# Pacing the preparation of entries in a neighbour-quantile kernel: late steps made good, first entries at shorter distances, sorts begun with the lists

## The chip, the cores and the metric

The kernel runs on one core of a Trainium2 chip, with its engines TensorE (PE), VectorE (DVE), ScalarE (ACT), GpSimd (POOL) and SyncE (SP, which issues transfers). The metric is the device time of one execution in microseconds; lower is better.

## The reference, cut to what matters

There are 16 graphs ("entries") of 1024 nodes with 64 features. Four layers follow each other, each with a residual and a layer norm:

```python
x = ln(x + mlp0(x, adj @ x))            # layer 0: tanh MLP on node and message
x = ln(x + (adj / deg) @ x)             # layer 1
x = ln(x + mlp2(x + quantiles(x, nd)))  # layer 2
x = ln(x + mlp3(x + quantiles(x, nd)))  # layer 3

# nd: neighbours left after a dilation; every skip-th neighbour of a node is removed, both ways
sv  = sort(where(nd, x[None], big))     # per node and feature, over its neighbours
agg = 0.25 * q(sv, .25) + 0.5 * q(sv, .5) + 0.25 * q(sv, .75)   # interpolated between two ranks
```

A node keeps between 1 and 33 neighbours, itself included. The neighbour set depends on the adjacency alone, so layers 2 and 3 use the same lists.

## The kernel before, in words

**Preparation of an entry b.** Three generators write its instructions piece by piece.

- `features` (L403) loads `x` and the adjacency, computes layers 0 and 1 (TensorE tiles `px`, `pd`, `pa`), makes the 0/1 matrix `near` on VectorE, writes the features to a table in DRAM and splits them into three bf16 parts. It sets `e.near`, then `e.parts[0]`.
- `lists` (L488) counts ranks with matmuls (`pr`), finds the removed neighbours (`takes`, then `e.taken`), sorts the nodes of the entry by their number of neighbours (`order`), packs the neighbour numbers (`pk`, then `e.packed`), and takes the largest eight at a time into the lists `e.idx` (`best`, `idx`; then `e.listed`).
- `ordered` (L634) is started by `lists` once `order` is there. It puts the features into node order (`e.xs[0]`, tile `x2s`), makes `place` and `none` for the longest lists, the quantile weights `e.wts`, and a check of the list lengths whose last instruction writes `over`.

**Rounds.** `sort_round(k)` handles layer 2 of entry k and layer 3 of entry k-2 together; there are 18 rounds, and rounds 0, 1, 16 and 17 have only one of the two. Nodes stand in eight tiles of 128, in the order of their list length. For seven of the tiles GpSimd gathers neighbours from the table with indirect transfers into a ring of 72 slots (`got_s`, by `fetch`, L886). For the eighth and longest, TensorE picks them with one-hot matrices (`fill`, L726: `hot` on VectorE, `pgk` on TensorE). VectorE sorts every tile with a network of min and max (`got`, `other`). `weigh` (L753) multiplies by `e.wts` and sums up; it also marks the ring slots as free. `finish_round` (L908) runs the MLP of the finished layers; the results of layer 2 are scattered to a second table and read back by `read_back` (L814).

**Order of the work.** On VectorE, ScalarE and TensorE the program's order is the one in which Python writes the instructions; GpSimd and SyncE are ordered by the scheduler of the compiler. `Weave` (L825) decides the order. Its clock is the planned VectorE time so far (`Metered`, L193: 0.13 us and a share by size for each instruction) and time skipped. A generator yields the distance to its next step in these microseconds. After every sort instruction `catch_up` takes the steps that are due. `step` sets the next due time:

```python
work[0] = max(self.now() - work[2], work[0]) + next(work[1])   # work[2] is the lag
```

With a lag of 0 the next distance counts from the moment at which the step was taken; with a lag of 4.0 (only `fill` has one) from its due time, as long as it was less than 4 us late. If a round needs something that is not there, `advance` takes the next step at once, whatever its due time, and the clock jumps.

`prepare` (L872) starts `features(b)` when entry b-1 has its `taken` and b is at most two past the current round, and `lists(b)` when b-1 is `listed`. A round's sorts of entry k are written only when `ready(k)` (L882): all three generators of the entry have ended.

Of the kernel before, what the change touches and what calls it, by code (L numbers as in the profile page):

```python
# [12 lines left out]
F32 = mybir.dt.float32  # L13
# [8 lines left out]
P = 128  # L22
# [190 lines left out]
def adj_resnorm_kernel(ctx: ExitStack, tc: tile.TileContext, x, adj_t, nodemask, w01, b01, w02, b02,  # L213
                       w21, b21, w22, b22, w31, b31, w32, b32, out):
    nc = tc.nc
    B, N, C = x.shape
    NT = N // P
# [3 lines left out]
    s = SimpleNamespace()  # L221
# [78 lines left out]
    most_wanted = max(len(want) for want in wants)  # L300
    want_ids = const.tile([P, NT, most_wanted], F16, name="want_ids")
    nc.gpsimd.memset(want_ids, NEVER)
    for t, want in enumerate(wants):
        for first, m, stride, length in regular_runs(want):
            for r in range(m):
                k = first + r * stride
# [178 lines left out]
        yield from split(x2, parts, y)  # L485
        e.parts[0] = parts

    def lists(b, e):  # L488

        while e.near is None:  # L490
            yield 2
# [3 lines left out]
        half = s.work.tile([P, NT], I32, name="nb_half", bufs=1)  # L495
        m, dil, lim, cut_at = st[:, 0], st[:, 1], st[:, 2:4], st[:, 4:6]
# [57 lines left out]
        own = s.work.tile([P, NT, 3], F16, name="own", bufs=1)  # L554
# [37 lines left out]
        order = s.sets.tile([P, NT, N], BF, name="order", tag="takes")  # L592
        for t in range(NT):
            dve.tensor_scalar(order[:, t, :], slot, key[:, 2, t : t + 1], None, op0=ALU.is_equal)
            if t % 3 == 2:
                yield 2
        preparing[b].append(weave.add(ordered(b, e, order, own)))


        e.idx = s.feat.tile([P, NT, KS], I32, name="idx", bufs=5)  # L600
# [33 lines left out]
    def ordered(b, e, order, own):  # L634
# [49 lines left out]
        e.place = place  # L684

        e.none = s.feat.tile([KW - 1, P], BF, name="none", bufs=5)
        e.wts = s.feat.tile([P, NT, most_wanted], F32, name="wts", bufs=5)
        for h in range(NH):
            half = slice(h * G, (h + 1) * G)
            pn = s.psum.tile([P, G, P], F32, name="pn", tag="s", bufs=1)  # L690
            for q in range(G):
                nc.tensor.transpose(pn[:KW, q, :], sorted_own[:, h * G + q, :1].to_broadcast([P, KW]), ident)
            yield 7
            counted = s.work.tile([KW, G, P], F32, name="counted", bufs=1)
            dve.tensor_scalar(counted, pn[:KW], nth[:KW], None, op0=ALU.is_equal)
            if h == NH - 1:
                dve.tensor_scalar(e.none, pn[: KW - 1, G - 1, :], nth[: KW - 1], BIG, op0=ALU.is_le, op1=ALU.mult)
            pw = s.psum.tile([P, G, most_wanted], F32, name="pw", tag="s", bufs=1)
            for q in range(G):
                nc.tensor.matmul(pw[:, q, :], counted[:, q, :], weights[:KW, h * G + q, :], start=True, stop=True)  # L700
            yield 9
            nc.scalar.copy(e.wts[:, half, :], pw)

        pc = s.psum.tile([P, HALF], F32, name="pc", tag="s", bufs=1)
        nc.tensor.transpose(pc[:NT, :P], count, ident)
# [16 lines left out]
    def members(k):  # L722

        return [(m, b, entries[b]) for m, b in enumerate((k, k - 2)) if 0 <= b < B]

    def fill(k):  # L726

        while k and (k - 1, NT - 1) not in free:
            yield 1
        t = NT - 1  # L730
        size = SIZES[t]
        got = tails[k] = s.lists.tile([P, 2, size, C], F32, name="got", tag="got_l", bufs=1)
        for m, b, e in members(k):
            while e.parts[m] is None or e.xs[m] is None or e.place is None or e.none is None:
                yield 1
            nc.scalar.copy(got[:, m, 0, :], e.xs[m][:, t, :])
            for g in range(1, size, 8):
                pg = s.psum.tile([P, 8, C], F32, name="pgk", tag="f", bufs=1)
                for i in range(g, g + 8):
                    hot = s.lists.tile([P, NT, P], BF, name="hot", bufs=HOTS)  # L740
                    dve.tensor_scalar(hot, e.place, float(i), None, op0=ALU.is_equal)
                    whole = i < LEAST[t]
                    if not whole:
                        nc.tensor.matmul(pg[:, i - g, :], e.none,
                                         ident_b[: KW - 1, i - 1 : i].to_broadcast([KW - 1, C]), start=True, stop=False)
                    pick(pg[:, i - g, :], hot, e.parts[m], whole)
                    yield 2.1
                yield 2
                nc.scalar.copy(got[:, m, g : g + 8, :], pg)
                yield 0.5  # L750
            e.filled[m] = True

    def weigh(k, t, got, agg, which):  # L753

        want = wants[t]
        prods = got[:, :, : len(want), :]
        for i, slot_id in enumerate(want):
            for m, b, e in members(k):
                nc.scalar.activation(prods[:, m, i, :], got[:, m, slot_id, :], AF.Copy, scale=e.wts[:, t, i : i + 1])  # L759
            if i % 6 == 5:  # L760
                yield 3
        yield 13
        left = len(want)
        while left > 2:
            more = left // 2
            dve.tensor_add(prods[:, which, :more, :], prods[:, which, :more, :], prods[:, which, left - more : left, :])
            left -= more
        dve.tensor_add(agg[:, which, t, :], prods[:, which, 0, :], prods[:, which, 1, :])
        free.add((k, t))
# [55 lines left out]
    class Weave:  # L825
# [5 lines left out]
        def now(self):  # L831
            return dve.us + self.skipped

        def add(self, gen, lag=0.0):

            self.works.append([self.now(), gen, lag])
            return gen

        def step(self, work):
            try:  # L840
                work[0] = max(self.now() - work[2], work[0]) + next(work[1])
            except StopIteration:
                self.works.remove(work)

# [15 lines left out]
        def finish(self, gen):  # L860
            while self.runs(gen):
                self.advance()

    entries = [SimpleNamespace(near=None, taken=False, packed=False, listed=False, there=None, place=None, none=None,
                               parts=[None, None], xs=[None, None], filled=[False, False]) for _ in range(B)]
    weave = Weave()
    preparing, tails = {}, {}
    free, gots, room, holders = set(), [], [0], [None] * ROOM
    allowed = [1]
    order_of_tiles = [(k, t) for k in range(B + 2) for t in reversed(range(NT - 1))]  # L870
# [1 line left out]
    def prepare():  # L872

        for b in range(B):
            while b > allowed[0] or (b and not entries[b - 1].taken):
                yield 2
            preparing[b] = [weave.add(features(b, entries[b]))]
            while b and not entries[b - 1].listed:
                yield 2
            preparing[b].append(weave.add(lists(b, entries[b])))  # L880

    def ready(b):  # L882

        return len(preparing.get(b, ())) == 3 and not any(weave.runs(gen) for gen in preparing[b])

    def fetch(must=-1):  # L886

# [27 lines left out]
    def sort_round(k):  # L915

        if k >= 2:
            weave.finish(rounds[k - 2])
        filling = weave.add(fill(k), lag=4.0)
        first = members(k)[0][0]  # L920
        which = slice(first, first + len(members(k)))
        agg = s.feat.tile([P, 2, NT, C], F32, name="agg")
        sums = []
        for t in (*reversed(range(NT - 1)), NT - 1):
            if t == NT - 1:
                weave.finish(filling)
                got = tails[k]
            else:
                n = order_of_tiles.index((k, t))
                fetch(n)  # L930
                got = gots[n]
            other = s.lists.tile([P, 2, SIZES[t], C], F32, name="other", bufs=1)
            pair = got[:, which], other[:, which]
            for is_max, d, v, i, j, to in usual[t]:
                dve.tensor_tensor(cut_pair(pair[to], v, d if is_max else 0), cut_pair(pair[i], v),
                                  cut_pair(pair[j], v, d), op=ALU.max if is_max else ALU.min)
                weave.catch_up()
                fetch()
            if len(sums) >= 2:
                weave.finish(sums[-2])  # L940
            sums.append(weave.add(weigh(k, t, got, agg, which)))
            weave.catch_up()
        if k:
            weave.finish(rounds[k - 1])
        rounds.append(weave.add(finish_round(k, agg, sums)))

    with ExitStack() as main:
        s.feat = main.enter_context(tc.tile_pool(name="feat", bufs=2))
        s.work = main.enter_context(tc.tile_pool(name="work", bufs=2))
        s.sets = main.enter_context(tc.tile_pool(name="sets", bufs=1))  # L950
        s.lists = main.enter_context(tc.tile_pool(name="lists", bufs=1))
        s.psum = main.enter_context(tc.tile_pool(name="psum", bufs=1, space=bass.MemoryType.PSUM))
        engines = mybir.EngineType
        main.enter_context(tc.manual_schedule(engines={engines.DVE, engines.Activation, engines.PE}))
        weave.add(prepare())
        rounds = []
        ring = s.lists.tile([P, 2, ROOM, C], F32, name="got_s")
        for k in range(B + 2):
            allowed[0] = k + 2
            sort_round(k)  # L960
        for gen in rounds:
            weave.finish(gen)


    def layernorm(dst, y):
# [216 lines left out]
    with tc.If(nc.values_load(over_d[:, B:]) > 0):  # L1182
        with tc.For_i(0, B) as b:
            with tc.If(nc.values_load(over_d[:, ds(b, 1)]) > 0), ExitStack() as general:
# [9 lines left out]
                wts = s.feat.tile([P, NT, LONG], F32, name="wts")  # L1194
# [62 lines left out]
```

## Time and profile before

| | |
|---|---|
| device time, median of 3 runs | 5359.1 us (5350.06 to 5362.13) |
| span of the profiled run | 5360.1 us |
| mean granted TensorE clock | 0.754 |
| busy: DVE / PE / POOL / ACT | 4448.2 / 3801.1 / 3665.9 / 2309.6 us |
| indirect gathers on POOL | 2944, 1143 ns in the mean |
| `hot` on DVE | 1024 instructions, 438 ns in the mean |

Busy time is the time in which an engine executes; waits are not in it. Because three engines are written in a fixed order, an instruction that waits holds back all that stand behind it on its engine. VectorE's instructions all bear the line of the metering helper (L207), so they are told apart by the tile that they write. The ends of rounds 0 to 3, seen at the last `agg<-got` of each, are at about 411, 729, 1140 and 1450 us, round 14 ends at 4764, and rounds 15, 16 and 17 end at 5021, 5138 and 5319.

The times of the first four entries, of one tile each (first start to last end, us):

| tile, engine | entry 0 | entry 1 | entry 2 | entry 3 |
|---|---|---|---|---|
| `px`, PE | 22 to 53 | 141 to 192 | 365 to 436 | 688 to 755 |
| `takes`, DVE | 129 to 137 | 351 to 362 | 672 to 682 | 961 to 972 |
| `pk`, PE | 180 to 226 | 428 to 483 | 748 to 800 | 1051 to 1103 |
| `idx`, DVE | 198 to 233 | 447 to 489 | 767 to 807 | 1087 to 1127 |
| `over`, DVE (end) | 267 | 556 | 871 | 1166 |

### The profile page before, as it was taken

What the parts mean: (1) busy time and instruction counts of PE and PEld (TensorE: products, weight loads), DVE (VectorE), ACT (ScalarE), POOL (GpSimd) and SP (SyncE); (2) the same over time, 40 slices, a digit from 0 to 9 for tenths busy, and PEclk for the clock granted to TensorE, in tenths of its full rate; (3) what the DMA queues carried; (4) which work ended last, traced back from release to release, by engine and by line L of the source; (5) the groups of instructions that cost most, each with busy time, mean ns of one, the idle gap of its engine ahead of it and who ended that gap; (6) DMA issues with size and microseconds to landing.
All of it is one profiled execution on the core that took longest, in us unless ns stands there. A gap on an engine that the chain in (4) does not pass through costs nothing.

```text
span 5360.1 us, 112278 instructions
## 1 busy us (share of the span) xinstructions
PE 3801.1 (71%) x45200; PEld 2956.6 (55%) x45304; DVE 4448.2 (83%) x8819; ACT 2309.6 (43%) x6102; POOL 3665.9 (68%) x3228
## 2 busy tenths in 40 slices
PE   6857476677786877878686887868686887744443
PEld 5735255466574756656564656656464656534332
DVE  2494666989899898989989898999899898989966
ACT  3343343536263544536353543636354553512222
POOL 0325725867878776777877776777768777777662
PEclk7878687788786877868687786868787786866555
DMA  2211212222222222222222222222211221111010
GB/s 82 71 36 41 53 39 56 54 55 59 54 46 54 45 57 56 57 59 58 54 44 46 52 55 56 58 56 50 63 45 43 55 57 43 26 23 25 18 25 10
DMA packets 420186, 259.37 MB, mean 48 GB/s; under 512 B 106164, under 2 KB 368452, under 8 KB 419652
## 3 DMA queue, kind: packets, MB, share of 16 engines
q0 software_dynamic: 102400, 105.06, 10.3%
q1 hardware_dynamic: 317252, 147.02, 9.8%
q8 instruction: 356, 5.83, 0.5%
q14 instruction: 178, 1.46, 0.1%
HBM read 239.27 MB, written 12.58 MB: 47 GB/s over the span
## 4 chain that ended last, share of the span: by engine, by line
DVE 57%; PE 24%; POOL 5%; ACT 5%; issue 4%; DMA 3%; DVEq 0%; SPq 0%; POOLq 0%; ACTq 0%
DVE other L207 19%; DVE got_s L207 13%; DVE got L207 9%; PE pgk L355 6%; POOL got_s L359 5%; DVE best L207 4%; DVE hot L207 3%; PE pr L522 3%; PE pa L464 3%; DVE less L207 3%; PE px L431 2%; DMA got_s<-table,idx 2%; ACT got L759 1%; PE pd L794 1%; PE pd L793 1%
## 5 line engine op out<-in xcount | busy, mean ns | idle before, releaser
L359 POOL DMA_INDIRECT got_s<-table,idx x2944 | 3365.5, 1143 | 1482.5 <-issue 741.6
L355 PEld LDWEIGHTS <-hot 128*128 128x128 bf16 x24576 | 909.2, 106 | 500.2 <-DVE hot L207 389.6
L355 PE MATMUL pgk<-x3p,hot 128*128 128x64 bf16 x12288 | 514.4, 206 | 335.6 <-DVE hot L207 234.6
L608 PE MATMUL pk<-near,order 128*128 128x512 f16 x2048 | 531.1, 416 | 128.5 <-DVE order L207 92.6
L207 DVE TENSOR_SCALAR hot<-place 128x1024 bf16<-128x1024 f16 x1024 | 444.7, 438 | 178.7 <-PE pgk L355 174.5
L207 DVE TENSOR_TENSOR other<-got_s 128x512 f32<-128x512 f32 (+8 forms) x900 | 515.2, 583 | 55.0 <-DMA got_s<-table,idx 27.3
L759 ACT ACTIVATE got_s<-got_s,wts 128x64 f32<-128x64 f32 x1568 | 400.4, 336 | 322.3 <-DVE got_s L207 309.6
L355 PE MATMUL pgk<-x2p,hot 128*128 128x64 bf16 x12288 | 491.2, 204 | 67.0 <-DVE hot L207 62.8
L207 DVE TENSOR_TENSOR got_s<-got_s 128x256 f32<-128x256 f32 (+7 forms) x918 | 490.9, 538 | 18.6
L464 PE MATMUL pa<-x,adj_r 128*128 128x65 f32 x2048 | 406.6, 385 | 95.2 <-DMA adj_r<-in_adj_dram 61.8
L464 PEld LDWEIGHTS pa<-x,adj_r 128*128 128x128 f32 x2048 | 397.5, 300 | 99.7 <-DMA adj_r<-in_adj_dram 62.5
L608 PEld LDWEIGHTS <-order 128*128 128x128 bf16 x2048 | 208.8, 105 | 413.4 <-DVE order L207 126.6
L207 DVE TENSOR_TENSOR got_s<-other 128x512 f32<-128x512 f32 (+8 forms) x774 | 408.6, 540 | 8.0
L522 PE MATMUL pr<-steps,near 128*128 128x512 bf16 x1432 | 374.0, 406 | 49.8 <-ACT junk L528 37.5
L207 DVE TENSOR_TENSOR other<-other 128x128 f32<-128x128 f32 (+13 forms) x558 | 318.6, 571 | 13.7
L431 PE MATMUL px<-adj_r,x_s 128*64 128x128 f32 x2048 | 288.2, 304 | 37.4 <-DMA adj_r<-in_adj_dram 22.2
L528 ACT ACTIVATE junk<-pr,nb_st 128x1024 f16<-128x1024 f32 x256 | 282.1, 1109 | 69.1 <-PE pr L522 69.1
L431 PEld LDWEIGHTS px<-adj_r,x_s 128*64 128x64 f32 x2048 | 263.0, 156 | 57.4 <-DMA adj_r<-in_adj_dram 23.2
L522 PEld LDWEIGHTS <-near 128*128 128x128 f16 x1536 | 151.9, 104 | 229.9 <-issue 95.6
L565 PE MATMUL pv<-minus_n,takes 128*128 128x128 bf16 x1024 | 206.4, 237 | 85.7 <-DVE takes L207 85.2
L759 ACT ACTIVATE got<-got,wts 128x64 f32<-128x64 f32 x672 | 163.8, 337 | 234.5 <-DVE got L207 234.5
L207 DVE TENSOR_TENSOR got<-got 128x1024 f32<-128x1024 f32 (+10 forms) x234 | 209.3, 895 | 44.4 <-ACT got L759 38.2
(204 smaller groups left out, 7257.6 us busy)
## 6 DMA issues: line engine op xcount, KB each, us to landing
adj_r<-in_adj_dram SPq DMA_DIRECT2D x256, 512.0 KB
got_s<-table,idx POOLq DMA_INDIRECT x2944
x_s<-in_x_dram SPq DMA_DIRECT2D x16, 256.0 KB
table<-x SPq DMA_DIRECT2D x16, 256.0 KB
x<-table SPq DMA_DIRECT2D x16, 256.0 KB
table<-x3s,rows POOLq DMA_INDIRECT x128
out_dram<-agg,out_rows POOLq DMA_INDIRECT x128
table<-no_row SPq DMA_DIRECT2D x6, 0.2 KB
```

Source lines behind the costliest of these rows:

```text
L207: return call(*args, **kwargs)
L355: nc.tensor.matmul(dst, hot[:, c, :], parts[:, c, q, :], start=first and c + q == 0, stop=c == NT - 1 and q == 2)
L359: nc.gpsimd.indirect_dma_start(out=dst, out_offset=None, in_=tab, in_offset=bass.IndirectOffsetOnAxis(ap=rows, axis=0))
L431: nc.tensor.matmul(px[C:, q * P : (q + 1) * P], x_s[:, jt, :], adj[t][:, jt, :], start=jt == 0, stop=jt == NT - 1)
L464: nc.tensor.matmul(pa[:, q, :], adj[i][:, jt, :], x1[:, jt, :], start=jt == 0, stop=jt == NT - 1)
L522: nc.tensor.matmul(pr[:, h * HALF : (h + 1) * HALF], near[:, c, t * P : (t + 1) * P], steps[:, ONSET + h * HALF - c * P :][:, :HALF], star ...
L528: nc.scalar.activation(junk, prs[t - 1], AF.Sign, bias=lim[:, i, t - 1 : t], scale=-1.0, accum_out=cut_at[:, i, t - 1 : t])
L565: nc.tensor.matmul(pv[:, cols], takes[:, c, rows], minus_n, start=False, stop=False)
L608: nc.tensor.matmul(cols, order[:, c, t * P : (t + 1) * P], left(c, slice(h * G, (h + 1) * G)), start=c == 0, stop=c == NT - 1)
L759: nc.scalar.activation(prods[:, m, i, :], got[:, m, slot_id, :], AF.Copy, scale=e.wts[:, t, i : i + 1])
L793: nc.tensor.matmul(pd[:, q, :], h_t[:, q * P : (q + 1) * P], w2s, start=True, stop=False)
L794: nc.tensor.matmul(pd[:, q, :], ones_row, bias_rows[1 + layer], start=False, stop=True)
```

## The change

It has four parts. Works get a lag and a pace: the three generators of an entry have a lag of 1.5 us, so that a step that comes late pulls the next ones forward, and the distances are multiplied by a pace. The pace is 0.6 for entries 0 to 3 and 1.0 for the others; fills keep their lag of 4.0 and have a pace of 0.7 in rounds 0 to 2. An entry is ready when its lists and its ordered features are there; `weigh` waits for the weights, which may now come later, and `e.wts` is set when both halves are written. At the end all works left are taken, not the rounds alone.

```diff
-    def lists(b, e):
+    def lists(b, e, pace):
...
-        preparing[b].append(weave.add(ordered(b, e, order, own)))
+        weave.add(ordered(b, e, order, own), 1.5, pace)
...
+        e.wts = wts
...
     def weigh(k, t, got, agg, which):
 
         want = wants[t]
+        while any(e.wts is None for m, b, e in members(k)):
+            yield 1
...
-        def add(self, gen, lag=0.0):
-
-            self.works.append([self.now(), gen, lag])
+        def add(self, gen, lag=0.0, pace=1.0):
+
+            self.works.append([self.now(), gen, lag, pace])
             return gen
...
-                work[0] = max(self.now() - work[2], work[0]) + next(work[1])
+                work[0] = max(self.now() - work[2], work[0]) + work[3] * next(work[1])
...
-            preparing[b] = [weave.add(features(b, entries[b]))]
+            pace = 0.6 if b < 4 else 1.0
+            weave.add(features(b, entries[b]), 1.5, pace)
...
-            preparing[b].append(weave.add(lists(b, entries[b])))
+            weave.add(lists(b, entries[b], pace), 1.5, pace)
...
-        return len(preparing.get(b, ())) == 3 and not any(weave.runs(gen) for gen in preparing[b])
+        return entries[b].listed and entries[b].xs[0] is not None
...
-        filling = weave.add(fill(k), lag=4.0)
+        filling = weave.add(fill(k), 4.0, 0.7 if k < 3 else 1.0)
...
-        for gen in rounds:
-            weave.finish(gen)
+        while weave.works:
+            weave.advance()
```

More of the change, by code (lines that the diff above doesn't have):

```diff
@@ L686, in ordered @@
         e.none = s.feat.tile([KW - 1, P], BF, name="none", bufs=5)
-        e.wts = s.feat.tile([P, NT, most_wanted], F32, name="wts", bufs=5)
+        wts = s.feat.tile([P, NT, most_wanted], F32, name="wts", bufs=5)
         for h in range(NH):
@@ L701, in ordered @@
             yield 9
-            nc.scalar.copy(e.wts[:, half, :], pw)
+            nc.scalar.copy(wts[:, half, :], pw)
+        e.wts = wts
         pc = s.psum.tile([P, HALF], F32, name="pc", tag="s", bufs=1)
@@ L864, in adj_resnorm_kernel @@
     entries = [SimpleNamespace(near=None, taken=False, packed=False, listed=False, there=None, place=None, none=None,
-                               parts=[None, None], xs=[None, None], filled=[False, False]) for _ in range(B)]
+                               wts=None, parts=[None, None], xs=[None, None], filled=[False, False]) for _ in range(B)]
     weave = Weave()
-    preparing, tails = {}, {}
+    tails = {}
     free, gots, room, holders = set(), [], [0], [None] * ROOM
```

## The prediction, made before the change was run

> **What bounds the kernel now.** I read the slices of the page first, then busy times in windows cut at the ends of the rounds (each ends with the `agg<-got` of its longest tile), then GpSimd's waits in order of time, then VectorE's timeline at one round's end.
>
> ```profile
> span 5360.1 us, 112278 instructions
> ...
> DVE  2494666989899898989989898999899898989966
> ...
> POOL 0325725867878776777877776777768777777662
> ```
>
> VectorE is 90% busy from slice 7 on, but only 40 to 60% busy in most of the first seven (940 us).
>
> ```profile
> 0.00:199.00 199.00, 148.66 (x1074) 115.78 (x1077) 40.97 (x142) 80.21 (x149) 5.47 (x28) 0.79 0.27 77
> 199.00:411.00 212.00, 135.11 (x1604) 98.77 (x1601) 169.78 (x442) 92.24 (x215) 91.86 (x92) 0.80 0.19 48
> 411.00:729.00 318.00, 180.88 (x1973) 130.68 (x1974) 186.07 (x472) 112.02 (x266) 162.48 (x161) 0.74 0.20 46
> 729.00:1140.00 411.00, 290.00 (x3359) 218.05 (x3368) 310.42 (x570) 161.97 (x403) 263.77 (x233) 0.79 0.21 50
> ...
> 1756.00:2048.00 292.00, 227.10 (x2778) 176.16 (x2784) 269.87 (x504) 144.03 (x380) 229.68 (x200) 0.77 0.22 51
> 2048.00:2360.00 312.00, 245.50 (x2873) 194.55 (x2881) 274.87 (x516) 144.58 (x384) 233.27 (x200) 0.77 0.24 55
> ```
>
> Columns: stretch, length, busy PE, PEld, DVE, ACT, POOL, clock, DMA. The rows are the time before the first gather, rounds 0, 1, 2, and rounds 5 and 6. Round 1 has half the sorting of a full round, and VectorE is busy for 186 of its 318 us. Round 2 is a full round and takes 411 us where later ones take about 302. So rounds 0 to 2 hold the waste; in rounds 5 and 6 VectorE idles 22 and 37 us.
>
> ```profile
> 447.65 0.94 POOL L359 DMA_INDIRECT got_s<-table,idx  x1 [112.54 <-DVE idx L207]
> ...
> 767.44 0.94 POOL L359 DMA_INDIRECT got_s<-table,idx  x1 [107.43 <-issue]
> ```
>
> GpSimd stands still for 112.5 us until entry 1's lists come, and for 107.4 us until entry 2's do (the `idx` of entry 2 is first written at 767). After 1140 its idle time is 844 us in 3624, nearly all of it the 0.3 us between two gathers: about 2400 of them are 720, which leaves some 124 us, 10 a round. So GpSimd is 97% taken in the steady part.
>
> ```profile
> 2048.40 0.29 DVE L207 TENSOR_TENSOR agg<-got 128x128 f32<-128x128 f32 x1
> ...
> 2061.56 0.59 DVE L207 TENSOR_SCALAR hot<-place 128x1024 bf16<-128x1024 f16 x1 [5.87 <-PE pgk L355]
> ...
> 2066.65 0.14 DVE L207 CAST over<-mf 1x1 int32<-1x1 f32 x1
> 2067.02 0.56 DVE L207 TENSOR_TENSOR other<-got_s 128x384 f32<-128x384 f32 x1 [0.23 <-ACT got_s L903]
> ```
>
> The last preparation instruction of entry 6 is `over<-mf`; the first sort of round 6 follows it by 0.4 us, 18 us after round 5 ended. The same pair stands at 1759.12 and 1759.39, and at 2666.45 and 2666.72 (3 us after the round). Each round therefore begins when `ordered` ends. Why `ordered` ends then is planned: I add the distances (the yielded numbers) from one `taken` to the next. `features` until `near` is whole: 8 + 2 x 50 + 4 + 26 (`settle`) + 2 x 23 + 5 = 189; `lists` until `taken`: 12 + 5 + 9 x 4.2 + 5 + 10 x 1.3 = 73. That is 262 in about 70 steps. The last `takes` of entries 4 to 15 end from 1254 to 4578, (4578 - 1254)/11 = 302 us apart. The excess, 40/70 = 0.57 us per step, is the lateness of a step that is looked for only after a sort instruction of 0.3 to 1.6 us. Preparation paces the steady part by a hair, with VectorE and GpSimd close behind.
>
> **What the Trainium skill says.** "Perfetto Trace Analysis", section Tensor Engine Instruction, says that ACT, DVE and GPSIMD are strict FIFO. So a preparation step put earlier can hold the sorts behind it; the trace agrees (`hot<-place` waits 5.87 us for PE above, and the sorts with it). "SBUF — State Buffer", section SBUF: two separate sides, says that GpSimd is locked out of the port pair it shares with VectorE in some VectorE operations and then can't write descriptors. The trace fits: a gather takes 940 ns at the shortest, but 1143 in the mean. The extra 0.2 us each won't vanish with better order, since the VectorE work stays. "TensorE: Matmul & The Clock Gate", part 1, says that activity releases the throttle; here the clock is 0.58 to 0.60 in the last rounds with PE 41 to 56% busy, and 0.77 in rounds 5 and 6. Denser preparation shouldn't lower it.
>
> **The change part by part.** No instruction is added or removed; only the order on VectorE, ScalarE and TensorE moves, so every cost is a wait.
>
> (a) Distances 0.6 for entries 0 to 3 (and 0.7 in the fills of rounds 0 to 2). Entry 0 runs alone: its `takes` end at 137 and `idx` is first written at 198, bound by engine latencies, and I change nothing there. Entry 1's distances from `taken` to the first `idx` are 189 + 73 + 67 (until `order`) + 20 = about 350; at 0.6, 210. What the engines need is seen in entry 0: from `pa` (68) to the last `idx` (233) is 165 us. Near tiles of entry 1 wait for `packed` of entry 0 (226), so its first `idx` can come at 226 + 130 = 356; with sorts between I take 370 instead of 447. The last follows at about 415 instead of 489. Later entries repeat a loop of 155 to 165 us alone; I take 185 with the sorts of rounds 0 and 1 between. So entry 2 has its first `idx` at 555 instead of 767 and entry 3 at 740 instead of 1087. The two waits of GpSimd shrink from 220 to about 50.
>
> (b) Sorts begin with the lists. Round 0's first sort comes at about 233 instead of 267, round 1's at 415 instead of 556, round 2's at about 600 instead of 871. A new wait: `weigh` waits for `wts`, some 50 us later in the plan; sorts of the first two tiles, about 25 us each, hide most of it. A late `weigh` frees its ring slots late, so GpSimd waits; 72 slots against the 65 of the first four tiles bound this at a few us.
>
> (c) Is there room? VectorE's work from 199 to 1140 is 170 + 186 + 310 = 666 us. At its steady share of 90% that takes 740 us, so round 2 could end at 940. GpSimd: 486 instructions at 1.45 us with their gaps are 705, plus 50 of waits: 955. I take 970 instead of 1140: 170 us saved.
>
> (d) The steady part: steps up to 1.5 us late are made good. The period of preparation falls from 302 towards 262 to 266, and `ready` no longer waits for the 50 us between the last `idx` and `mf` (2012 and 2066). Preparation stops pacing; each entry then waits for the round that allows it. The round is bound by VectorE's 272 us plus waits that stay (hot on PE 140 us in 12 rounds, adjacency 84, small ones 83, so 26 a round), 298, and by GpSimd's 302 - 10 = 292. I take 296, 6 us in each of 12 rounds: 72 us. Unknown is what a step that comes up to 1.5 us sooner adds in VectorE waits. Bounds: nothing, or 0.3 us in some 30 of the VectorE steps that follow a ScalarE or TensorE result, 9 us a round.
>
> (e) Rounds 15 to 17 have no preparation left; finishing all works at the end changes nothing. Zero.
>
> Sum: 5359 - 170 - 72 = 5117, rounded to 5120.
>
> **The rivals.** A: only the start gains. For it: GpSimd is 97% taken from 1140 on. Against: its idle 10 us a round are mostly waits for sorts at the round's start. Start 170, steady 0: 5190. B: both parts reach their floors. For it: VectorE's 272 leave room. Start 200, steady 10 x 12 = 120: 5040. Against: it needs GpSimd without a wait. C, the other side: shortened distances make VectorE stand in line for ScalarE and TensorE, and the moved phase puts `pa` and `px` beside the fills' `pgk`; 9 us a round are 108, the start gains only 70: 5400. For it: `hot` already waits 140 us for PE in the steady part, and `near` 34 us for adjacency at 549. Against: in the start VectorE is idle anyway, 130 us of round 1 alone.
>
> **How the numbers follow.** Forecast 0.45, A 0.27, B 0.15, C 0.09, and 0.04 for a start that gains 60 with nothing after it (5300). The time is the likeliest, 5120. The low end goes under B, to 5000, as the start may gain more than 200 if the loop runs at its 160 us. The high end of 5290 covers A with a start of half the size and some lost waits. Faster by over 0.2%: 0.45 + 0.27 + 0.15 + 0.02 = 0.89; slower 0.08; same 0.03.
>
> **What would show it.** Right: first `idx` of entries 1, 2, 3 near 370, 555 and 740; GpSimd's two long waits together under 60 us; round 2 ends near 970; rounds 3 to 14 about 296 us apart, with a sort before `over<-mf`; VectorE's busy sum unchanged at 4450. Wrong: if first `idx` times hardly move, engines, not distances, set the start; if the steady rounds stay at 302, GpSimd was the pace; if `hot<-place` and `near` waits grow by over 100 us, C is at work.

## The result and the profile after

The changed kernel takes 5411.5 us in the median (5403.5 to 5413.1), the kernel before 5360.6 in the same comparison: a ratio of 1.0096, 95% interval 1.0079 to 1.0114. It is slower by 1%, where 4.5% less time was forecast.

From the page of the changed kernel, the same three lines as before:

```profile
span 5411.4 us, 112427 instructions
...
DVE  2487777989898897878889787887978789979966
...
POOL 0335476877777576767768677776867768777562
```

```profile
201.00:497.00 296.00, 242.97 (x2423) 178.09 (x2420) 238.39 (x594) 131.79 (x315) 171.21 (x166) 0.80 0.27 65
497.00:743.00 246.00, 202.98 (x2082) 149.71 (x2079) 188.82 (x464) 136.76 (x301) 123.13 (x118) 0.81 0.23 55
743.00:1076.00 333.00, 226.04 (x2871) 173.79 (x2871) 275.00 (x508) 143.54 (x363) 245.36 (x205) 0.77 0.22 52
2005.00:2322.00 317.00, 242.82 (x2831) 184.21 (x2831) 272.47 (x509) 142.58 (x379) 235.94 (x203) 0.77 0.22 51
2322.00:2640.00 318.00, 243.92 (x2831) 185.70 (x2831) 273.11 (x511) 143.05 (x381) 228.90 (x198) 0.77 0.22 51
```

These are busy times of the changed kernel in windows cut at its own rounds (columns PE, PEld, DVE, ACT, POOL, clock, DMA): rounds 0, 1, 2, and then 6 and 7. Round 2 ends at 1076 instead of 1140 and round 3 at 1379 instead of 1450: the start gained some 70 us. But rounds 6 and 7 take 317 and 318 us for the same 272 to 273 us of VectorE's work. From the end of round 6 to that of round 13 the period is 317.5 us, against 303.3 before. Between the ends of rounds 3 and 13 that is 3165 us instead of 3033, 132 more; less the 71 of the start and some 10 in the last rounds, it is the loss of 51.

GpSimd's two long waits in the changed kernel, in order of time:

```profile
392.47 0.94 POOL L359 DMA_INDIRECT got_s<-table,idx  x1 [62.18 <-DVE idx L207]
...
608.31 0.94 POOL L359 DMA_INDIRECT got_s<-table,idx  x1 [51.97 <-ACT code L619]
```

They fell from 220 us to 114. VectorE's timeline at the start of round 7, and where the check of entry 7 ends:

```profile
2321.74 0.29 DVE L207 TENSOR_TENSOR agg<-got 128x128 f32<-128x128 f32 x1
...
2323.37 0.61 DVE L207 TENSOR_TENSOR other<-got_s 128x256 f32<-128x256 f32 x2
...
2503.66 0.14 DVE L207 CAST over<-mf 1x1 int32<-1x1 f32 x1
```

The stop between rounds is gone: the first sort comes 1.6 us after the last sum. Entry 7's `over` was written long before, in round 6 (at 2186); the one at 2503.66 is that of entry 8. Preparation now runs well ahead of the sorts: the rounds no longer wait for `ordered`. What took the place of that wait stands in the waits of VectorE, first before, then after, over the whole span (total us, times, longest):

```profile
DVE hot L207 <- PE pgk L355: 174.5, 95, 9.8
```

```profile
DVE hot L207 <- PE pgk L355: 392.8, 169, 7.3
```

VectorE makes the one-hot matrices of the fill in four buffers (`HOTS` in the kernel), so a fifth must wait until TensorE has used the first. TensorE in the changed kernel, in order of time, during one of these waits:

```profile
2374.38 1.56 PE L355 MATMUL pgk<-x2p,hot 128*128 128x64 bf16 x48
2375.87 0.20 PE L745 MATMUL pgk<-ident_b,none 32*128 32x64 bf16 x1
2376.00 0.87 PE L355 MATMUL pgk<-x2p,hot 128*128 128x64 bf16 x24
2376.80 1.96 PE L431 MATMUL px<-adj_r,x_s 128*64 128x128 f32 x16
2379.51 1.56 PE L355 MATMUL ordered_x<-x2p,order 128*128 128x64 bf16 x48 [0.74 <-ACT sorted_own L643]
2380.90 3.62 PE L608 MATMUL pk<-near,order 128*128 128x512 f16 x16
2384.45 1.12 PE L789 MATMUL ph<-o_t,w21s 64*128 64x512 f32 x2
2385.50 0.20 PE L745 MATMUL pgk<-ident_b,none 32*128 32x64 bf16 x1
2385.63 0.87 PE L355 MATMUL pgk<-x2p,hot 128*128 128x64 bf16 x24
```

and VectorE at the same time:

```profile
2381.13 0.17 DVE L207 COPY mask_s<-sorted_own 128x8 f32<-128x8 f32 x1
2386.55 0.43 DVE L207 TENSOR_SCALAR hot<-place 128x1024 bf16<-128x1024 f16 x1 [5.25 <-PE pgk L355]
2386.89 0.68 DVE L207 TENSOR_TENSOR other<-other,got_s 128x512 f32<-128x512 f32 x1
```

Between two picks of the fill, from 2376.80 to 2385.50, stand `px` of entry 9, `ordered_x` and `pk` of entry 8, and `ph` of a finished round (1.1 us): 8.7 us. VectorE waits 5.25 us for a buffer, and the sort behind the `hot` waits with it. In windows of round 7 (here the stretch of these waits, and the last part of the round):

```profile
2362.00:2425.00 63.00, 62.26 (x863) 43.06 (x861) 38.54 (x67) 17.09 (x37) 41.54 (x43) 1.00 0.25 57
...
2502.00:2639.00 137.00, 75.80 (x612) 50.08 (x608) 132.95 (x224) 82.18 (x211) 109.58 (x91) 0.74 0.22 53
```

For 63 us TensorE is 99% busy, at a granted clock of 1.00, and VectorE 61%; later in the round VectorE is 97% busy and TensorE 55%. TensorE's matmuls are the same as before; it is busy with them for 243 us a round here and 234 before (means of rounds 7 to 13). What changed is their place. Before, `pr`, `pv` and some `px` stood beside the fill, and `pk` and `ordered_x` after it. In round 7, `pk` of entry 8 began 178 us after the end of round 6 before, and 37 us after it now; `px` of entry 9 began 105 us after it, and now 15 us ahead of it.

### The profile page after: what moved, and what is told of

The parts are those of the page before. It is cut to its first block, busy times and chain, and to the rows that moved or that the text cites. A ratio compares the mean times of both kernels' runs of the same rounds, so it can differ in the third digit from the quotient of the medians.

```text
span 5411.4 us, 112427 instructions
## 1 busy us (share of the span) xinstructions
PE 3883.9 (72%) x45304; PEld 2975.3 (55%) x45304; DVE 4454.0 (82%) x8819; ACT 2295.4 (42%) x6086; POOL 3677.3 (68%) x3228
## 4 chain that ended last, share of the span: by engine, by line
DVE 48%; PE 40%; issue 3%; ACT 3%; POOL 3%; DMA 2%; DVEq 0%; POOLq 0%; ACTq 0%
DVE other L207 18%; DVE got_s L207 12%; PE pgk L355 10%; DVE got L207 9%; PE pk L608 8%; PE pa L464 5%; PE px L431 3%; DVE hot L207 2%; POOL got_s L359 2%; DMA got_s<-table,idx 2%; PE ordered_x L355 2%; PE pd L797 1%; PE pd L796 1%; PE pd L449 1%; PE pd L448 1%
## 5 line engine op out<-in xcount | busy, mean ns | idle before, releaser
L355 PEld LDWEIGHTS <-hot 128*128 128x128 bf16 x24576 | 949.0, 108 | 595.5 <-DVE hot L207 514.3
L355 PE MATMUL pgk<-x3p,hot 128*128 128x64 bf16 x12288 | 563.0, 215 | 251.7 <-DVE hot L207 182.6
L522 PE MATMUL pr<-steps,near 128*128 128x512 bf16 x1536 | 483.5, 486 | 346.1 <-ACT junk L528 190.5
L355 PE MATMUL pgk<-x2p,hot 128*128 128x64 bf16 x12288 | 477.2, 201 | 252.6 <-DVE hot L207 229.3
L608 PE MATMUL pk<-near,order 128*128 128x512 f16 x2048 | 478.4, 389 | 0.0
L565 PE MATMUL pv<-minus_n,takes 128*128 128x128 bf16 x1024 | 239.5, 259 | 250.0 <-DVE takes L207 248.9
L464 PE MATMUL pa<-x,adj_r 128*128 128x65 f32 x2048 | 376.8, 362 | 49.5 <-ACT x L385 26.9
L464 PEld LDWEIGHTS pa<-x,adj_r 128*128 128x128 f32 x2048 | 361.4, 275 | 74.4 <-ACT x L385 27.2
L565 PEld LDWEIGHTS <-takes 128*128 128x128 bf16 x1024 | 118.3, 116 | 422.7 <-DVE takes L207 278.5
L564 PE MATMUL pv<-scaled,near 128*128 128x128 f16 x1024 | 240.9, 260 | 138.1 <-ACT near L569 137.8
L750 ACT COPY got<-pgk 128x512 f32<-128x512 f32 x128 | 74.7, 584 | 546.6 <-PE pgk L355 546.6
```

The source lines that it names most:

```text
L355: nc.tensor.matmul(dst, hot[:, c, :], parts[:, c, q, :], start=first and c + q == 0, stop=c == NT - 1 and q == 2)
L464: nc.tensor.matmul(pa[:, q, :], adj[i][:, jt, :], x1[:, jt, :], start=jt == 0, stop=jt == NT - 1)
L522: nc.tensor.matmul(pr[:, h * HALF : (h + 1) * HALF], near[:, c, t * P : (t + 1) * P], steps[:, ONSET + h * HALF - c * P :][:, :HALF], star ...
L564: nc.tensor.matmul(pv[:, cols], near[:, c, rows], scaled[:, c, :], start=True, stop=False)
L565: nc.tensor.matmul(pv[:, cols], takes[:, c, rows], minus_n, start=False, stop=False)
L608: nc.tensor.matmul(cols, order[:, c, t * P : (t + 1) * P], left(c, slice(h * G, (h + 1) * G)), start=c == 0, stop=c == NT - 1)
```

## The experiments

Theories, as stated ahead of the runs: **P**, the lag lets preparation overtake the rounds until the gate of two entries (`features` of entry b begins at the start of round b-2 at the soonest) stops it, so that it starts at each round's start and `pk` falls among the fill. **R**, the earlier start of the sorts does the harm. **D** and **S**, the shortened distances themselves do it, at the start or through the lag. **G**, any later start of `features` helps, whatever then stands beside the fill.

All kernels that ran on chips where the kernel before takes about 5360 us, with the two of the case. The end of round 3 shows the start; period is the time from the end of round 6 to that of round 13, by seven; "hot" is VectorE's wait in `hot` for `pgk` in that stretch, per round; GpSimd is its idle time in pieces over 0.5 us, per round; the last column counts the larger groups of preparation's matmuls between the first and last `pgk` of round 7. These columns are worked out from the traces, the ratios are to the kernel before on the same chip.

| kernel | us | ratio (95%) | round 3 ends | period | hot | GpSimd | beside the fill of round 7 |
|---|---|---|---|---|---|---|---|
| before | 5359 | 1 | 1450 | 303.3 | 13.2 | 9.0 | pr 88, pv 192, px 64 |
| after | 5411 | 1.0096 (1.0079 to 1.0114) | 1379 | 317.5 | 31.2 | 25.5 | pk 128, ordered_x 192, px 80, pa 96 |
| lag alone | 5390 | 1.0056 (1.0036 to 1.0077) | 1431 | 313.8 | 26.1 | 25.3 | pk 128, ordered_x 192, px 128, pv 192, pa 16 |
| ready alone | 5277 | 0.985 (0.9834 to 0.9866) | 1416 | 294.8 | 1.4 | 0.7 | pa 112, pr 96, pv 24 |
| paces alone | 5224 | 0.9755 (0.9739 to 0.9771) | 1318 | 304.0 | 13.6 | 8.9 | pr 88, pv 192, px 64 |
| lag for entries 0 to 3 only | 5189 | 0.9686 (0.9669 to 0.9702) | 1387 | 288.4 | 1.5 | 0.3 | pa 96, pr 96, pv 48 |
| gate at tile 5 | 5327 | 0.994 (0.9923 to 0.9956) | 1357 | 314.4 | 27.6 | 19.9 | pk 128, ordered_x 192, px 128, pv 192, pr 33 |
| gate at tile 3 | 5169 | 0.9652 (0.9636 to 0.9668) | 1314 | 294.4 | 3.6 | 2.1 | pr 96, pv 192, px 64, pa 16 |
| gate at tile 2 | 5180 | 0.9668 (0.9652 to 0.9684) | 1275 | 296.3 | 3.0 | 2.2 | pr 89, pv 192, px 32, pa 96 |
| gate at tile 3, no paces | 5281 | 0.9856 (0.984 to 0.9872) | 1439 | 295.5 | 3.6 | 2.5 | pr 89, pv 192, px 64, pa 32 |
| gate at tile 3, lag for 0 to 3 only | 5195 | 0.969 (0.9674 to 0.9707) | 1296 | 293.1 | 1.6 | 0.0 | pa 128, pr 88 |
| all but the lag | 5101 | 0.9517 (0.9501 to 0.9533) | 1274 | 292.6 | 1.2 | 0.0 | pa 128, pr 88 |

**Runs on two other chips.** The first runs of four kernels fell on a chip on which the kernel before took 7090 us, and those of three gates and a second run of the paces alone on one on which it took 7152 us. The waits of the paces alone, on the first:

```profile
PEld L355 <- issue: 1080.5, 1260, 14.8
...
DVE hot L207 <- remote: 759.1, 104, 34.4
PE pgk L355 <- issue: 740.8, 1002, 15.2
```

There TensorE stands for about a thousand microseconds in "issue", that is, for nothing that the profile shows (the same kernel, on a chip where the kernel before takes 5360, has 54.1 us in the first line). With such stops these times can't be set beside those of this case, so the four kernels and the three gates were run again on chips where the kernel before takes about 5360 us. The first ratios were 1.0392 (lag alone), 1.0254 (ready alone), 0.991 and 1.0006 (paces alone, twice), 1.0188 (lag for entries 0 to 3), 1.0679 (gate at tile 5), 1.0316 (gate at tile 2) and 1.0062 (gate at tile 3, no paces). Their expectations:

> The kernel before with the lag of 1.5 us for the three preparation generators alone. Theory P (the lag lets preparation overtake the rounds until the gate of two entries holds it; it then starts at each round's start, and its packing matmuls pk fall among the fill's hot): steady period about 317 us as after, little gain at the start, so 5440 to 5540 us. Theory R (the earlier start of the sorts does the harm, the lag alone relieves the pacing): period at most 302, 5250 to 5350 us.

> The changed kernel with every lag of preparation 0 and every pace 1.0, so that only the earlier ready, the wait for wts and the end differ from before. Theory P: steady period about 302 us, a start gain of 30 to 100 us, 5260 to 5330 us. Theory R: period near 317 us, 5450 to 5550 us.

> The changed kernel with every lag of preparation 0 and the old ready, so that only the paces 0.6 and 0.7 of the start differ. Theories P and R: steady period 302 us, start gain about 70 us, 5270 to 5310 us. Theory D (the shortened distances of the first entries shift the phase for good): period over 310, 5400 us or more.

> The changed kernel with the lag of 1.5 us kept for entries 0 to 3 and 0 for the later ones. Theory P: the start as after (round 3 ends near 1379), then a period of about 302 us, 5270 to 5310 us. Theory R: the period stays near 317 us, about 5410 us.

> The changed kernel with the gate moved too, but only past the sorting of tile 5 (the second one). In the written order the fill then has pv, px, pk and ordered_x of preparation beside it, about 155 us of TensorE's work against 106 in the changed kernel and 107 with the gate at tile 3. Theory P: the fill is longer and VectorE waits more for it, period 320 us or more, 5420 us or more, slower than the changed kernel. Theory G (any start of features after the round's first moments helps, whatever then stands beside the fill): period near 296 us, 5170 to 5250 us.

> The changed kernel with the gate past the sorting of tile 2 (the fifth one): pr, pv and three quarters of pa beside the fill, pk and most of px outside. Theory P: VectorE waits little for the fill, and with the gathers as the next limit the period is 292 to 300 us: 5140 to 5210 us. Theory G: the same, or slower if preparation comes too late for its round (over 5250).

> The gate at tile 3 with all paces 1.0: only the shorter distances of the start are taken away. If these are what gains at the start, round 3 ends near 1420 instead of 1314 and the time is 5250 to 5290 us; if lag and ready do it alone, within 20 us of 5169.

> The changed kernel with no lag of preparation and the old ready, so only the paces of the start are left. Theory P: period near 302 us as before (preparation paces, pr and pv beside the fill), start gain 50 to 100 us: 5260 to 5310 us. Theory D (the shortened distances shift the phase for good): period over 310, 5400 us or more.

**One part alone.** The lag alone, in the kernel before:

```diff
-            preparing[b] = [weave.add(features(b, entries[b]))]
+            preparing[b] = [weave.add(features(b, entries[b]), 1.5)]
...
-            preparing[b].append(weave.add(lists(b, entries[b])))
+            preparing[b].append(weave.add(lists(b, entries[b]), 1.5))
```

(and so for `ordered`.)

> The kernel before with the lag of 1.5 us alone[...]. Theory P: it drifts to the order of the changed kernel by about round 8 and then has its period of 317 us; 5400 to 5480 us. Theory R (the earlier start of the sorts does the harm): period at most 302, 5250 to 5350 us.

Measured: 5390, just under P's band. Its rounds show the drift: the periods of rounds 4 to 6 are 303, 303 and 300, those from round 11 on 319, 317 and 317. R falls: the lag alone is slower than before, with the old `ready`. The lag brought next to nothing even before the drift was complete; by round 7 `pk` already stood beside the fill.

Ready alone, in the changed kernel:

```diff
-            weave.add(features(b, entries[b]), 1.5, pace)
+            weave.add(features(b, entries[b]), 0.0, pace)
...
-            pace = 0.6 if b < 4 else 1.0
+            pace = 1.0
```

(and so for `lists` and `ordered`; the fills' pace 1.0.)

> The changed kernel with no lag of preparation and paces of 1.0, so only the earlier ready is left; in the written order the fill then stands beside pa and pr. Theory P: preparation still paces at about 302 us and the start gains 30 to 100: 5260 to 5330 us. Theory R: period near 317 us, 5450 to 5550 us.

Measured: 5277, in P's band, but not for P's reason: the period fell to 294.8, where 302 was expected, and the start gained 34 at round 3. R falls a second time. The earlier `ready` is worth 8.5 us a round, and in it GpSimd hardly rests (0.7 us a round). It shifts the phase too: `pa` and `pr` stand beside the fill, and the wait in `hot` falls from 13.2 to 1.4 us. How much of the 8.5 us comes from which was not tried apart.

Paces alone, the changed kernel with lags of 0 and the old `ready`:

```diff
-            weave.add(features(b, entries[b]), 1.5, pace)
+            preparing[b] = [weave.add(features(b, entries[b]), 0.0, pace)]
...
-        return entries[b].listed and entries[b].xs[0] is not None
+        return len(preparing.get(b, ())) == 3 and not any(weave.runs(gen) for gen in preparing[b])
```

(and so for the other two.)

> Only the paces of the start, on such a chip. Theory P: period near 302 us, start gain 50 to 100 us: 5260 to 5310 us. Theory D (the shortened distances shift the phase for good): period over 310, 5400 us or more.

Measured: 5224, under the band of P: the period is 304.0 as P says, but the start gains 132 us at the end of round 3, more than its 100. D falls.

**Where the lag does its harm.** The lag kept for entries 0 to 3 only:

```diff
-            weave.add(lists(b, entries[b], pace), 1.5, pace)
+            weave.add(lists(b, entries[b], pace), 1.5 if b < 4 else 0.0, pace)
```

(and so for the other two.)

> The changed kernel with the lag of 1.5 us for entries 0 to 3 only. Theory P: start as after, then a period of about 302 us with pr and pv or pa beside the fill, 5270 to 5310 us. Theory R: period near 317 us, about 5410 us.

Measured: 5189, under the band of P. Round 3 ends at 1387 (1379 in the changed kernel), and the period is 288.4 instead of 302; a single short round, the seventh with 256 us, is in it, and rounds 8 to 13 take 293.9 in the mean. So the lag of the late entries makes the 317.

**The phase alone.** Everything as changed, the lag too, but `features` of an entry (from entry 3 on) may begin only after tile 3 of the round two before it has been sorted:

```diff
-    allowed = [1]
+    allowed = [2]
...
+            if t == 3:
+                allowed[0] = k + 2
...
-            allowed[0] = k + 2
             sort_round(k)
```

> The changed kernel with one edit: an entry's features may begin when tile 3 of the round two before it has been sorted, not at that round's start. In the written order this moves pk and ordered_x out of the fill and puts pr and pv beside it, as in the kernel before, with lag, pace and ready as changed. Theory P: the time at which TensorE is full and VectorE waits for it (2362 to 2425 of the changed kernel) goes, the steady period is at most 302 us, and with the start gain the time is 5260 to 5340 us. Theory S (the shorter distances themselves make VectorE wait, wherever preparation stands): period near 317 us, 5390 us or more.

Measured: 5169, under the band of P, and a period of 294.4. S falls: the same shortened distances do no harm once preparation stands elsewhere, with `pk` and `ordered_x` out of the fill. Busy time of this kernel in the fill of round 7 (columns as above), and its wait for `hot` there:

```profile
2230.00:2377.00 147.00, 132.89 (x2129) 107.86 (x2126) 140.25 (x312) 94.75 (x238) 113.23 (x105) 0.87 0.25 56
```

```profile
DVE hot L207 <- PE pgk L355: 2.5, 2, 1.5
```

The same two lines for the fill of round 7 in the changed kernel:

```profile
2322.00:2512.00 190.00, 178.12 (x2383) 145.06 (x2383) 148.81 (x308) 61.62 (x171) 126.45 (x115) 0.81 0.22 51
```

```profile
DVE hot L207 <- PE pgk L355: 31.3, 12, 5.8
```

The fill takes 147 us instead of 190, with VectorE 95% busy instead of 78%.

The gate at tile 5 and at tile 2:

```diff
-            if t == 3:
+            if t == 5:
```

(and `t == 2`.)

> The gate past tile 5[...]. Theory P: with about 155 us of preparation's TensorE work beside the fill (106 in the changed kernel), period 320 us or more, 5420 us or more. Theory G (any later start of features helps): period near 296 us, 5170 to 5250 us.

> The gate past tile 2, on such a chip. Theory P: pk stays out of the fill, VectorE waits little for it, and with the gathers as the next limit the period is 292 to 300 us: 5140 to 5210 us. Theory G: the same, or over 5250 if preparation comes too late for its round.

Measured: 5327 and 5180. The gate at tile 2 lies in P's band, and G allows it too; the gate at tile 5 tells them apart. G falls: a start of `features` two tiles into the round, with `pk` still beside the fill, keeps a period of 314.4 us. Its wait in the fill of round 7:

```profile
DVE hot L207 <- PE pgk L355: 28.0, 12, 7.5
```

It is 85 us faster than the changed kernel all the same; 21 of these lie between the ends of rounds 6 and 13, the rest at the start and the end. P's size was wrong here: it asked for 320 us and more, since some 155 us of preparation's matmuls should stand beside the fill against 106. These two figures came from the written order, and the traces don't bear them out. TensorE's busy time in that fill, to be set beside the 178.12 and 132.89 us above:

```profile
2276.00:2465.00 189.00, 166.28 (x2494) 131.10 (x2498) 151.66 (x314) 92.38 (x207) 145.11 (x137) 0.91 0.22 49
```

Counted from the first to the last `pgk` of a round, in the mean of rounds 7 to 13, preparation keeps TensorE busy for 91 us in the changed kernel, for 89 with the lag alone and with the gate at tile 5, and for 45 to 56 in all the others (54 with the gate at tile 3). So the like waits of 28 and 31 us go with like amounts of work. The kernels with a period of over 313 us are those with about 90 us of preparation there, and also those with `pk` and `ordered_x` there together with `px`; no other kernel is either. Whether the amount decides or the kind was not tried apart; part of the amount may also follow from the fill's being longer. `px` alone doesn't do it: 64 of its matmuls stand there before and with the gate at tile 3 as well.

**The start.** The gate at tile 3 with all paces 1.0:

```diff
-            pace = 0.6 if b < 4 else 1.0
+            pace = 1.0
...
-        filling = weave.add(fill(k), 4.0, 0.7 if k < 3 else 1.0)
+        filling = weave.add(fill(k), 4.0, 1.0)
```

> The gate at tile 3 with all paces 1.0, on such a chip. If the shorter distances are what gains at the start, round 3 ends near 1420 instead of 1314 and the time is 5250 to 5290 us; if lag and ready do it alone, within 20 us of 5169.

Measured: 5281, and round 3 ends at 1439: without the paces, lag and `ready` gain 11 us at the start. Most of the gain of the start is that of the paces.

**All but the lag.** The changed kernel with 0.0 in place of 1.5 in all three generators:

```diff
-            weave.add(features(b, entries[b]), 1.5, pace)
+            weave.add(features(b, entries[b]), 0.0, pace)
```

> The changed kernel without its lag: paces of the start and the earlier ready stay, every lag of preparation is 0. In the written order pa and pr stand beside the fill in the steady part, pk never. Theory P: the start of the paces alone (round 3 ends near 1318) and the period of ready alone (about 295 us): 5110 to 5170 us. If the lag had its own use at the start, round 3 ends later than 1340 and the time is 5180 to 5230.

Measured: 5101, faster than both kernels of the case and 9 us under the band of P: a ratio of 0.9517 (0.9501 to 0.9533) to the kernel before. Its page:

```profile
span 5109.2 us, 112335 instructions
...
DVE  2498978999998988999989988999989989898966
```

and GpSimd's waits in it from 1300 to 4500 us:

```profile
POOL got_s L359 <- issue: 427.6, 1403, 0.3
POOL got_s L359 <- DMA got_s<-table,idx: 91.5, 300, 0.3
```

No wait of GpSimd there is longer than 0.3 us: the gathers are now the pace. Round 3 ends at 1274, 105 us sooner than with the lag, so the lag cost something at the start as well: round 0 ends at 497 in the changed kernel and at 434 here.

The gate at tile 3 with the lag for entries 0 to 3 only, beside the gate's edit:

```diff
-            weave.add(features(b, entries[b]), 1.5, pace)
+            weave.add(features(b, entries[b]), 1.5 if b < 4 else 0.0, pace)
```

> The gate at tile 3, with the lag for entries 0 to 3 only. Theory P: start as with the gate at tile 3 (round 3 ends near 1314), period 289 to 295 us: 5100 to 5165 us.

Measured: 5195, a miss of 30 us. Period 293.1 as expected, but rounds 4 and 5 took 326 and 279 us, and round 5 ends at 1901 against 1823 without any lag or gate. The early entries' lag doesn't gain: with the old gate, too, it is slower with that lag than without any (5189 against 5101).

## Why the prediction was wrong

- **What bounds the kernel.** Right in what it named: GpSimd close to its limit (292 us a round estimated; 293 to 296 measured in the kernels in which it hardly rests, the short round above left out), VectorE at 272 (272.6 in the changed kernel), and rounds that begin when `ordered` ends. The claim that preparation paces the rounds is only half shown: the earlier `ready` alone brought 8.5 us a round, but it moved the phase as well, and the lag alone brought nothing.
- **(a), the start.** First `idx` of entries 1, 2 and 3 came at 392, 607 and 813 instead of 370, 555 and 740. The loop takes 215 and 206 us, not 185; this term was too small, and the waits of GpSimd came to 114 instead of 50. The paces alone end round 3 at 1318, 132 sooner; with `ready` and no lag round 2 ends at 999 and round 3 at 1274, 142 and 176 sooner. So most of the 170 us that (c) put at the end of round 2 was there to be had, without the lag. With it the changed kernel had 65 there; the gate at tile 2 ended round 3 at 1275 with the lag too, but lost it in a round 4 of 352 us.
- **(b), the sorts with the lists.** Right only for round 0, whose first sort comes at 243 (233 forecast; 273 before). Those of rounds 1 and 2 come at 500 and 744 instead of 415 and 600 (560 and 875 before; the `over` times in the table of the first four entries are 3 to 4 us too low; they are 271, 560, 875 and 1169). They follow the end of the round before them by 4 and 1 us, so they no longer wait for `ordered`, but for that round: round 0 now takes 296 us instead of 212, with 238 us of VectorE's work in it instead of 170, since preparation pulled forward is written among its sorts. (b) left this out. What the new wait for `wts` costs isn't shown: it moves the place of instructions and is no wait of an engine by itself.
- **(d) is the step that failed.** It said that "each entry then waits for the round that allows it", which is what happened, and gave that no price. Preparation that waits for the round's start has a fixed phase: `px` of entry k+2, `pk` and `ordered_x` of entry k+1 stand beside the fill of round k, and the wait in `hot` rose from 13.2 to 31.2 us a round. The period came to 317.5 us instead of 296. Without the lag it is 292.6, and with the lag kept and the gate moved to tile 3 it is 294.4.
- **The sum in (d)** took VectorE's waits as 26 us a round that "stay". They didn't: VectorE's whole idle time between the ends of rounds 6 and 13 is 31.5 us a round before and 44.9 in the changed kernel, though the wait for the adjacency (7.4 us a round before) went away. With the lag kept and the gate at tile 3 the idle time is 22.4. GpSimd's 292 us don't help when it waits 25.5 us a round, most of it (18.9) for VectorE's sorts to free ring slots. The sum was loose by itself, too: the 296 that it takes lie under its own 298 for VectorE, and the idle time before was 31.5 and not 26, so that with waits that stay VectorE alone fills the old period.
- **The bounds of the unknown in (d)**, 0 to 9 us a round, were for steps that come 1.5 us too soon. The gate at tile 3, with the same lag, shows no such cost; the cost lay in the 120 to 140 us by which preparation moved within the round (`px` of entry 9 and `pk` of entry 8 above). A bound on a wrong mechanism gave a range that was too narrow.
- **Rival C** was the one that came true, at 0.09. It named the phase and the waits of `hot`. Of its sign, `hot` and `near` waiting over 100 us more, `hot` gave 218 us, while `near` fell by 150 (from 167.5 to 17.0). Its start gain of 70 was met (71 at the end of round 3), its 9 us a round were 14; its pair was `pa` and `px`, the traces show `pk`, `ordered_x` and `px`. What stood against it, idle VectorE time at the start, says nothing on the steady part.
- **(e)** and the count of VectorE's work (4454 against 4450) were right.

## What to carry to other kernels

When several streams share engines in a fixed order, relieving one that paces doesn't only remove a wait: it lets that stream run to its next gate, and the gate decides what it then stands beside. Ask of a planner's change not how much sooner the steps come but where they end up, and count, in the order of the engine that serves it, what lies between two instructions of the stream with few buffers. Measure the parts of a joint change apart: here the change without its lag gains 4.8%, and the lag takes it all back.

## What was not expected of the hardware

On two chips the kernel before took 7090 and 7152 us instead of about 5360. In the traces from there, the weight loads of one line (L355) stood in "issue" for 1080.5 us (paces alone) and 1541.8 us (gate at tile 5); the same two kernels have 54.1 and 71.9 us on the other chips. The ratios don't carry over: the paces alone are 0.9755 where the kernel before takes 5360, and 0.991 and 1.0006 on these; ready alone is 0.985 and 1.0254. What TensorE waited for there stays open.

A gather takes longer beside a busy VectorE. In the kernel before, the 292 gathers during which VectorE stood still (busy for under a tenth of the gather) took 0.94 us in the mean and 0.99 at the most; the 1963 during which it was busy for over four fifths, mostly with `TENSOR_TENSOR`, took 1.21 in the mean. That agrees with the 0.2 us that the prediction set aside; what causes it was not tried apart.
